# Layer 2's shifted rows in transfers of 60, 2 and 63 rows, long shifts first, and its fourth ring cleared by ScalarE

## The chip, the cores and the metric

The kernel runs on one core of one Trainium2 chip. The metric is the device time of one execution in microseconds. A core has TensorE (PE; its weight loads are listed as PEld), VectorE (DVE), ScalarE (ACT), GpSimd (POOL) and SyncE (SP). In this kernel SP issues nearly all direct transfers, which 16 DMA engines carry out.

## The reference

Four layers follow each other on x of shape (4, 256, 64, 64), float32. Each takes the group-normalized x and adds its result to x:

```
x = x + L0(gn(x))   # modulated deformable 3x3 convolution
x = x + L1(gn(x))   # attention over the 4096 places
x = x + L2(gn(x))   # DCNv4: sampled 3x3 windows in 16 groups of 16 channels
x = x + L3(gn(x))   # a Mamba block, scanned along the 4096 places
```

The change lies in layer 2:

```
xp   = einsum('bchw,oc->bhwo', x, w_value) + b_value
off, mask = split(einsum('bchw,oc->bhwo', x, w_om) + b_om)    # 9 points a group
val  = bilinear samples of the zero-padded xp at (y + ky + off_y, x + kx + off_x)
out  = einsum('bhwkgc,bhwgk->bhwgc', val, mask)
x   += einsum('bhwc,oc->bohw', out, w_out) + b_out
```

## The kernel before

Images go one after the other, and within an image the layers too. Layer 2 takes no gather. It assumes that no offset is over one place (a flag sends the program to another version else), so each output place needs only the 5 x 5 places around it. For every place and group a table `A` of 5 x 5 weights is built from mask and offsets, and the output is the sum of 25 products of weights and shifted values.

The 128 partitions hold two half images: partition 64h + x is column x of half h. Rows are taken two at a time, in 16 steps p (`T = 2`). The projected values of two rows (a "ring" of shape 128 x 5 x 2 x 256) are made by PE (`values`, L754 and L756). Then `spread` copies them by ACT into the middle of five places (L762), and fills the other four by transfers from SBUF to SBUF that shift by d = -2, -1, 1, 2 partitions within each half (L766). A shift by 1 moves 63 partitions, a shift by 2 moves 62, each with one contiguous row of 2 KB, so a spread has eight transfers. The partitions that a shift leaves out must hold zero, which is why the four rings are cleared at the start of each image's layer 2: two by POOL (L739), the third by ACT (L741), the fourth by POOL (L945).

Step p uses rings p, p+1 and p+2. Three spreads go out at the start, ring p+3 is spread during step p, and the last one, ring 17, during step 14. Step p does, for the five window rows wy and two rows t:
- `product` (L888 on DVE, L893 on POOL): DVE multiplies five places at once for t = 0 and wy < 4, and otherwise three (shifts -2, -1, 0), with POOL doing the other two (shifts 1, 2);
- `shares` (L875, L876) on ACT, a copy of weights for POOL's part;
- for the next step `masked` (L803), `outer` (L823, on POOL) and `gather` (L836), which build the next `A`;
- `pairs` (L902) on POOL, one addition, and `total` (L913) on PE, which sums the remaining places by transposes into PSUM.

`project` (L852) and `finish` (L864) on PE and DVE close a step two steps later.

PE, ACT, DVE and POOL keep the order in which the code of the steps is written (`manual_schedule`), so a waiting instruction holds up all that stands behind it on its engine. What stands before that block, such as the normalization (`scaled`, L201, on DVE) and the clearing of the first three rings, is put into order by the framework. SP issues transfers in order, too. Eight completion semaphores take turns on SP, and an issue waits until the transfer eight places earlier has landed.

Of the kernel before, what the change touches and what calls it, by code (L numbers as in the profile page):

```python
# [63 lines left out]
class Net:  # L64
# [635 lines left out]
    def layer2(self, x):  # L700
# [3 lines left out]
        nc, tc = self.nc, self.tc  # L704
        gk, T = GRP * K2, 2
        with (
# [27 lines left out]
            ring = []  # L734
            for i in range(4):

                r = pa.tile([P, WIN, VR, 256], F32, tag=f"ring{i}", name=f"ring{i}")
                if i < 2:
                    nc.gpsimd.memset(r, 0.0)  # L739
                elif i == 2:  # L740
                    nc.scalar.copy(  # L741
                        r.rearrange("p x y c -> p (x y c)"), zero.to_broadcast([P, WIN * VR * 256])
                    )
                ring.append(r)

            def values(q, pool=None):

                r = ring[q % 4]
                pc = pool.tile([P, 512], F32, tag="pacc", name="pc3") if pool else self.ps("pc2")
                for u in range(VR):  # L750
                    y = VR * q + u
                    o = pc[:, bass.ts(u, 256)]
                    for ct in range(2):
                        nc.tensor.matmul(o, xr[:, ct, y, :], wv[:, ct, :], start=(ct == 0), stop=False)  # L754
                    k = 1 if y < 2 else 2 if y >= HH + 2 else 0
                    nc.tensor.matmul(o, self.halves[:, k, :], bv, start=False, stop=True)  # L756
                return pc

            def spread(q, pc):

                r = ring[q % 4]
                nc.scalar.copy(r[:, 2].rearrange("p y c -> p (y c)"), pc)  # L762
                for d in (-2, -1, 1, 2):
                    for h in range(2):
                        a, b = 64 * h + max(0, -d), 64 * h + 64 - max(0, d)
                        nc.sync.dma_start(out=r[a:b, 2 + d, :, :], in_=r[a + d : b + d, 2, :, :])  # L766


            made = {}
# [1 line left out]
            def offsets(p, t):  # L771

                if t == 0:
                    made.setdefault(p, {})["po"] = pom.tile([P, T, 512], F32, tag="pom", name="pom")
                po = made[p]["po"]
                for ct in range(2):
                    nc.tensor.matmul(
                        po[:, t, : 3 * gk], xr[:, ct, T * p + t + 2, :], wom[:, ct, :], start=(ct == 0), stop=False
                    )
                nc.tensor.matmul(po[:, t, : 3 * gk], self.halves[:, 0, :], bom, start=False, stop=True)  # L780

            def hats(p, part):


                d = made[p]
                po = d["po"][:, :, : 2 * gk]
                if part == 0:
                    d["hat"] = pb.tile([P, 2 * gk, T, 3], F32, tag="hat", name="hat")
                    d["ab"] = pb.tile([P, T, 2 * gk], F32, tag="ab", name="ab", bufs=1)
                side = lambda i: d["hat"][:, :, :, i].rearrange("p k t -> p t k")  # L790
                if part == 0:
                    nc.scalar.activation(side(0), po, AF.Relu, scale=-1.0)
                    nc.scalar.activation(side(2), po, AF.Relu)
                    nc.scalar.activation(d["ab"], po, AF.Abs)
                else:
                    nc.scalar.activation(side(1), d["ab"], AF.Identity, bias=1.0, scale=-1.0)

                    nc.scalar.activation(d["ab"], d["ab"], AF.Relu, bias=-1.0, accum_out=seen[:, p : p + 1])

            def masked(p):  # L800
                d = made[p]
                d["mh"] = pb.tile([P, gk, T, 3], F32, tag="mh", name="mh")
                nc.vector.tensor_mul(  # L803
                    d["mh"],
                    d["hat"][:, 0:gk],
                    d["po"][:, :, 2 * gk : 3 * gk]
                    .rearrange("p t (k u) -> p k t u", u=1)
                    .to_broadcast([P, gk, T, 3]),
                )

            def clear(p):
                A = pshare.tile([P, 1024], F32, tag="A", name="A")[:, : GRP * T * WIN * WIN]
                nc.scalar.copy(A, zero.to_broadcast([P, GRP * T * WIN * WIN]))
                made.setdefault(p, {})["A"] = A.rearrange("p (g t y x) -> p g t y x", t=T, y=WIN, x=WIN)

            def outer(p, i, engine):

                d = made[p]
                if i == 0:
                    d["pr"] = pb.tile([P, gk * T, 3, 3], F32, tag="pr", name="pr", bufs=1)  # L820
                mh, hat = (d[n].rearrange("p k t i -> p (k t) i") for n in ("mh", "hat"))
                n = gk * T // 3
                engine.tensor_mul(  # L823
                    d["pr"][:, bass.ts(i, n)],
                    mh[:, bass.ts(i, n), :].rearrange("p k (y x) -> p k y x", x=1).to_broadcast([P, n, 3, 3]),
                    hat[:, bass.ds(gk * T + i * n, n), :]
                    .rearrange("p k (y x) -> p k y x", y=1)
                    .to_broadcast([P, n, 3, 3]),
                )
# [94 lines left out]
            with tc.manual_schedule(  # L924
                engines={
                    mybir.EngineType.PE,
                    mybir.EngineType.Activation,
                    mybir.EngineType.DVE,
                    mybir.EngineType.Pool,
                }  # L930
            ):
                clear(0)
                for t in range(T):
                    offsets(0, t)
                hats(0, 0)
                spread(0, values(0))
                hats(0, 1)
                spread(1, values(1, pacc))
                masked(0)
                for i in range(3):  # L940
                    outer(0, i, nc.vector)
                spread(2, values(2))
                for t in range(T):
                    offsets(1, t)
                nc.gpsimd.memset(ring[3], 0.0)  # L945
                for i in (0, 2, 1):
                    gather(0, i)
                hats(1, 0)
                hats(1, 1)


                behind = None
                for p in range(last + 1):
                    near, far = p < last, p < last - 1
                    for wy in range(WIN):
                        product(p, wy, 0)
                        if wy == 0:
                            shares(p)
                        if near and wy == 0:
                            masked(p + 1)  # L960
                        product(p, wy, 1)
                        if wy == 1 and p > 1:
                            finish(p - 2)
                        if near and wy > 1:
                            gather(p + 1, wy - 2)
                        if near and wy < 3:
                            outer(p + 1, wy, nc.gpsimd)
                        left = pairs(p, wy)
                        if behind:
                            total(*behind)  # L970
                        behind = p, wy, made[p]["prod"], left
                        if wy == 0:
                            if p:
                                turned(p - 1)
                            if near:
                                clear(p + 1)
                        if far and wy < 2:
                            offsets(p + 2, wy)
                        if wy == 2:
                            if far:  # L980
                                hats(p + 2, 0)
                            if p < last:
                                spread(p + 3, values(p + 3))
                        if wy == 3:
                            if far:
                                hats(p + 2, 1)
                        if wy == 4:
                            if p:
                                project(p - 1)
                total(*behind)  # L990
                nc.scalar.preload_act_table_set("sqrt_and_others")
                turned(last)
                finish(last - 1)
                project(last)
                finish(last)
# [853 lines left out]
```

## Time and profile before

| | |
|---|---|
| three runs | 9211.65, 9220.24, 9221.78 us, median 9220.24 |
| the profiled execution | 9224.37 us, its span 9222.6 us |
| granted TensorE clock | 0.967 |
| busy in the span | PE 8204.3 us (89%), DVE 7308.7 (79%), POOL 6976.5 (76%), ACT 4967.0 (54%) |
| layer 2, fourth image | from about 7916 to 8255 us of the span |
| L766, SP, ring<-ring | 576 transfers, 569/767/2512 ns min/median/max for an issue |
| L893, POOL | 384 instructions, median 1072 ns |
| L888, DVE | 640 instructions, 936 to 1492 ns |
| L739 and L945, POOL clearing a ring | 2231 ns each, and 2377 ns |
| L741, ACT clearing a ring | 2323 ns |

A line of the timeline gives the start and the length in us, the engine, the line of the kernel, the operation, the tiles written and read, their shapes and the number of instructions merged into it; in brackets stands the engine's idle time just before it and what ended that. "us" in the issue of a transfer is the time that it takes on SP, not the time until the data has landed. Shares of the whole span say little here, since the four layers have different limits; what bounds layer 2 has to be read in its own stretch.

### The profile page before, as it was taken

What the parts mean: (1) busy time and instruction counts of PE and PEld (TensorE: products, weight loads), DVE (VectorE), ACT (ScalarE), POOL (GpSimd) and SP (SyncE); (2) the same over time, 40 slices, a digit from 0 to 9 for tenths busy, and PEclk for the clock granted to TensorE, in tenths of its full rate; (3) what the DMA queues carried; (4) which work ended last, traced back from release to release, by engine and by line L of the source; (5) the groups of instructions that cost most, each with busy time, mean ns of one, the idle gap of its engine ahead of it and who ended that gap; (6) DMA issues with size and microseconds to landing.
All of it is one profiled execution on the core that took longest, in us unless ns stands there. A gap on an engine that the chain in (4) does not pass through costs nothing. (4 is left out here: it accounts for less than half of the span.)

```text
span 9222.6 us, 95498 instructions
## 1 busy us (share of the span) xinstructions
PE 8204.3 (89%) x32023; PEld 4337.2 (47%) x32023; DVE 7308.7 (79%) x8245; ACT 4967.0 (54%) x7717; POOL 6976.5 (76%) x4224
## 2 busy tenths in 40 slices
PE   5889898998888989899888898999988889889997
PEld 4643473443564346344356435634435633564443
DVE  5864498999786458999978645899997854689998
ACT  4843336666684333666668333366666833336664
POOL 4746697998674669799867467889986746788997
PEclk9999999999999999999999999999999999999999
DMA  8930011222892011122389101112248900111221
GB/s 301 356 120 1 29 58 59 67 67 82 288 360 90 1 34 61 56 66 66 100 297 359 61 1 39 59 57 67 66 121 311 349 33 1 43 61 53 63 63 51
DMA packets 409192, 1017.79 MB, mean 110 GB/s; under 512 B 38833, under 2 KB 106834, under 8 KB 406642
## 3 DMA queue, kind: packets, MB, share of 16 engines
q0 software_dynamic: 165888, 604.05, 17.5%
q1 hardware_dynamic: 242802, 407.54, 14.4%
q8 instruction: 255, 4.18, 0.2%
q14 instruction: 247, 2.02, 0.1%
HBM read 849.60 MB, written 88.10 MB: 102 GB/s over the span
## 5 line engine op out<-in xcount | busy, mean ns | idle before, releaser
L1704 POOL TENSOR_TENSOR h<-h,cn 128x2048 f32<-128x2048 f32 x508 | 2300.4, 4528 | 41.1 <-POOL carry L1701 0.2
L1681 DVE TENSOR_TENSOR_SCAN h<-da,carry,h 128x512 f32<-128x512 f32 x1800 | 2175.2, 1265 | 85.0 <-ACT da L1679 36.8
L1679 ACT ACTIVATE da<-delta,l3a 128x512 f32<-128x512 f32 x2048 | 1395.7, 689 | 1206.4 <-DVE h L1681 1202.7
L1561 PE MATMUL y<-h,ident 128*128 128x512 f32 x4096 | 1923.7, 603 | 14.8 <-POOL h L1704 14.8
L371 POOL DMA_INDIRECT g<-tab,idx x1152 | 1337.0, 1161 | 515.3 <-DVE r L380 131.3
L592 POOL TENSOR_TENSOR acc<-acc,e 128x1024 f32<-128x1024 f32 x480 | 1125.4, 2345 | 540.0 <-ACT e L588 518.8
L1561 PEld LDWEIGHTS y<-h,ident 128*128 128x128 f32 x4096 | 787.7, 194 | 1067.6 <-issue 975.9
L415 PE MATMUL pz<-cols,l0w 128*128 128x256 f32 x4608 | 1154.8, 395 | 30.2 <-DVE cols L404 24.5
L489 DVE TENSOR_REDUCE m<-pm 128x3 f32<-128x1536 f32 (+2 forms) x340 | 599.5, 1763 | 699.6 <-PE pm L479 699.6
L380 DVE SCALAR_TENSOR_TENSOR r<-g,wx,r 128x512 f32<-128x512 f32 x1152 | 862.2, 748 | 238.0 <-ACT r L379 230.5
L588 ACT ACTIVATE e<-sc 128x1024 f32<-128x1024 f32 x512 | 496.1, 1020 | 1029.4 <-PE sc L575 1025.2
L1598 DVE TENSOR_TENSOR h<-du,bn 128x2048 f32<-128x2048 f32 (+1 forms) x512 | 1025.9, 2004 | 4.0 <-PE bn L1583 3.9
L599 PE MATMUL cx<-e,v 128*128 128x512 f32 x2048 | 1000.2, 616 | 0.0
L379 ACT ACTIVATE r<-g,wx 128x512 f32<-128x512 f32 x1152 | 830.0, 720 | 283.1 <-DMA g<-tab,idx 230.9
L415 PEld LDWEIGHTS pz<-cols,l0w 128*128 128x128 f32 x4608 | 857.9, 196 | 179.3 <-DVE cols L404 79.4
L888 DVE TENSOR_TENSOR prod<-ring,A 128x768 f32<-128x768 f32 (+1 forms) x640 | 716.6, 1161 | 90.0 <-DMA ring<-ring 59.3
L913 PE MATMUL pacc<-ident,prod 128*128 128x128 f32 x5120 | 678.8, 284 | 75.7 <-POOL prod L893 41.7
L397 PE MATMUL pt<-ident,acc 128*128 128x128 f32 x2304 | 437.2, 290 | 264.3 <-DVE acc L388 261.3
L913 PEld LDWEIGHTS pacc<-ident,prod 128*128 128x128 f32 x5120 | 576.7, 144 | 164.9 <-POOL prod L893 62.2
L599 PEld LDWEIGHTS cx<-e,v 128*128 128x128 f32 x2048 | 352.3, 189 | 599.0 <-issue 596.4
L387 ACT ACTIVATE acc<-r,wy 128x256 f32<-128x256 f32 x1152 | 569.2, 494 | 4.2 <-DVE r L380 3.1
L388 DVE SCALAR_TENSOR_TENSOR acc<-r,wy,acc 128x256 f32<-128x256 f32 x1152 | 551.7, 479 | 2.4 <-ACT acc L387 2.0
(272 smaller groups left out, 11488.7 us busy)
## 6 DMA issues: line engine op xcount, KB each, us to landing
cn<-cd SPq DMA_DIRECT2D x512, 256.0 KB
bs<-cd SPq DMA_DIRECT2D x248, 256.0 KB
tab<-vtnext SPq DMA_DIRECT2D x96, 512.0 KB
ring<-ring SPq DMA_DIRECT2D x288, 126.0 KB
ring<-ring SPq DMA_DIRECT2D x288, 124.0 KB
g<-tab,idx POOLq DMA_INDIRECT x1152, 6.3
tab<-vt SPq DMA_DIRECT2D x28, 640.0 KB
x<-in_x SPq DMA_DIRECT2D x64, 256.0 KB
```

What stands on the lines that cost most here:

```text
L371: nc.gpsimd.indirect_dma_start(out=g[:], out_offset=None, in_=tab[:, :], in_offset=bass.IndirectOffsetOnAxis(ap=idx[:, t, k : k + 1], axis=0),
L379: nc.scalar.mul(r, g[:, :, 0, :], wx[:, 0, t, k : k + 1])
L380: nc.vector.scalar_tensor_tensor(r, g[:, :, 1, :], wx[:, 1, t, k : k + 1], r, ALU.mult, ALU.add)
L415: nc.tensor.matmul(sums[m][:, ot, :256], wf[:, i, bass.ts(ot, P)], cols[m][:, i, :], start=(i == 0), stop=(i == 17),)
L592: nc.gpsimd.tensor_add(b["acc"], b["acc"], e)
L599: nc.tensor.matmul(blocks[qb]["cx"], v[:, 4 * (i + kt // 4 * 4) + kt % 4, :], e[:, bass.ts(i % 2, 512)], start=(kt == 0 and i == 0), stop= ...
L913: nc.tensor.matmul(d["pd"][:, ct, t, :], prod[:, x, t, bass.ts(ct, P)], self.ident, is_transpose=True, start=(wy == 0 and x == left[0] and ...
L1561: nc.tensor.matmul(c["ys", dc], self.ident, h[:, dc, :], start=False, stop=(n == DS - 1))
L1598: nc.vector.tensor_mul(h[:, :d, :], c["du"][:, :d, :], c.pop(("bn", n)).to_broadcast([P, d, C]))
L1679: nc.scalar.activation(da, c["delta"][:, dc, :], AF.Exp, scale=al[:, dc, n : n + 1])
L1681: nc.vector.tensor_tensor_scan(h[:, dc, :], da, hb, carry[:, dc, n : n + 1], ALU.mult, ALU.add)
L1704: nc.gpsimd.tensor_mul(h, h, cn.to_broadcast([P, 4, C]))
```

## The change

The two shifts by 2 are each cut into one transfer of 60 partitions and one of 2, for both halves; the shifts by 1 stay as they were. A spread then has twelve transfers for eight. Both long shifts are issued ahead of the short ones. The fourth ring is cleared by the same ACT copy as the third, ahead of the block with the fixed order, and POOL's memset in that block is gone. In ACT's program the new copy stands behind the square root of the normalization (L189) and ahead of the first clearing of `A` (L813). Lines from L767 on move down by one, and those behind L945 stay.

```
@@ -737,7 +737,7 @@
                 r = pa.tile([P, WIN, VR, 256], F32, tag=f"ring{i}", name=f"ring{i}")
                 if i < 2:
                     nc.gpsimd.memset(r, 0.0)
-                elif i == 2:
+                else:
                     nc.scalar.copy(
                         r.rearrange("p x y c -> p (x y c)"), zero.to_broadcast([P, WIN * VR * 256])
                     )
@@ -760,10 +760,11 @@
 
                 r = ring[q % 4]
                 nc.scalar.copy(r[:, 2].rearrange("p y c -> p (y c)"), pc)
-                for d in (-2, -1, 1, 2):
+                for d in (-2, 2, -1, 1):
                     for h in range(2):
                         a, b = 64 * h + max(0, -d), 64 * h + 64 - max(0, d)
-                        nc.sync.dma_start(out=r[a:b, 2 + d, :, :], in_=r[a + d : b + d, 2, :, :])
+                        for lo, hi in ((a, b),) if d % 2 else ((a, a + 60), (a + 60, b)):
+                            nc.sync.dma_start(out=r[lo:hi, 2 + d, :, :], in_=r[lo + d : hi + d, 2, :, :])
 
 
             made = {}
@@ -942,7 +943,6 @@
                 spread(2, values(2))
                 for t in range(T):
                     offsets(1, t)
-                nc.gpsimd.memset(ring[3], 0.0)
                 for i in (0, 2, 1):
                     gather(0, i)
                 hats(1, 0)
```

More of the change, by code (lines that the diff above doesn't have):

```diff
@@ L739, in layer2 @@
                     nc.gpsimd.memset(r, 0.0)
-                elif i == 2:
+                else:
                     nc.scalar.copy(
@@ L762, in spread @@
                 nc.scalar.copy(r[:, 2].rearrange("p y c -> p (y c)"), pc)
-                for d in (-2, -1, 1, 2):
+                for d in (-2, 2, -1, 1):
                     for h in range(2):
                         a, b = 64 * h + max(0, -d), 64 * h + 64 - max(0, d)
-                        nc.sync.dma_start(out=r[a:b, 2 + d, :, :], in_=r[a + d : b + d, 2, :, :])
+                        for lo, hi in ((a, b),) if d % 2 else ((a, a + 60), (a + 60, b)):
+                            nc.sync.dma_start(out=r[lo:hi, 2 + d, :, :], in_=r[lo + d : hi + d, 2, :, :])
             made = {}
@@ L944, in layer2 @@
                     offsets(1, t)
-                nc.gpsimd.memset(ring[3], 0.0)
                 for i in (0, 2, 1):
```

## The prediction

> **What bounds the kernel now.** I read the busy shares first, then layer 2's stretch of the last image by windows, then GpSimd's instructions at both ends of it, then the DMA view. All four images look alike here, so the fourth stands for them.
>
> Stretches of layer 2: start, first rows, middle, end; columns are length, busy time of PE, PEld, DVE, ACT, POOL, the granted clock, the DMA share and GB/s:
>
> ```profile
> 7917.00:7933.00 16.00, 9.86 (x28) 5.25 (x28) 12.41 (x27) 8.00 (x10) 6.88 (x4) 0.68 0.19 69
> 7933.00:7980.60 47.60, 29.05 (x123) 18.00 (x122) 29.83 (x38) 14.38 (x23) 17.55 (x15) 0.78 0.24 78
> 7980.60:8193.00 212.40, 210.35 (x1307) 157.99 (x1305) 203.92 (x272) 86.49 (x147) 212.40 (x171) 1.00 0.19 59
> 8193.00:8251.00 58.00, 46.86 (x292) 37.92 (x291) 43.80 (x58) 10.68 (x21) 45.39 (x38) 0.91 0.14 43
> ```
>
> In the middle POOL is busy all 212.40 us: it is the bound, one pair of rows every 17.5 us, and no transfer is on the path. In the first 47.6 us it works 17.55 us. What it waits for, at the start and at the end:
>
> ```profile
> 7951.78 1.06 POOL L893 TENSOR_TENSOR prod<-ring,near 128x512 f32<-128x512 f32 x1 [27.91 <-ACT near L876]
> ...
> 7962.60 1.06 POOL L893 TENSOR_TENSOR prod<-ring,near 128x512 f32<-128x512 f32 x1 [6.79 <-DMA ring<-ring]
> ...
> 7975.08 1.06 POOL L893 TENSOR_TENSOR prod<-ring,near 128x512 f32<-128x512 f32 x1 [4.47 <-DMA ring<-ring]
> ...
> 7980.60 1.07 POOL L893 TENSOR_TENSOR prod<-ring,near 128x512 f32<-128x512 f32 x1
> ```
> ```profile
> 8236.07 1.28 POOL L902 TENSOR_TENSOR prod<-prod 128x512 f32<-128x512 f32 x1 [0.19 <-DVE prod L888]
> 8241.15 1.06 POOL L893 TENSOR_TENSOR prod<-ring,near 128x512 f32<-128x512 f32 x1 [3.81 <-DMA ring<-ring]
> ```
>
> DVE has such a wait of 7.25 us too, before its first product at 7949.83 (it is what delays 7951.78). So the shifted rows bound both ends, 4 times. Why they are slow, in the last spread alone (issued from 8224.55 to 8232.1):
>
> ```profile
> GB/s 0 0 0 0 26 0 0 0 0 23 16 66 92 82 108 157 118 82 128 134 92 46 52 52 49 52 46 52 49 52 49 26 13 0 0 0 0 0 0 0
> DMA packets 545, 1.04 MB, mean 42 GB/s; under 512 B 44, under 2 KB 44, under 8 KB 544
> ...
> ring<-ring SPq DMA_DIRECT2D x4, 126.0 KB
> ring<-ring SPq DMA_DIRECT2D x4, 124.0 KB
> ```
>
> 500 rows of 2 KB make 500 packets; the 44 small ones are completion marks, one per DMA engine and transfer: 4a + 4b = 44. The trace puts 2 marks on a 62-row transfer and 9 on a 63-row one, the largest divisors of 62 and 63 up to 16. For 6 us the queue runs at some 51 GB/s: two engines, 31 rows each, 0.080 us a row. All 62-row transfers sit on the same two engines: 4 x 31 + 4 x 7 = 152 rows, 12.2 us a spread. Three spreads back to back give the landings 7949.6, 7962.4, 7974.8, which are the waits above.
>
> Last, a collision ahead of all this:
>
> ```profile
> 7920.63 3.02 DVE L201 TENSOR_SCALAR xr<-x,gm,rs 128x256 f32<-128x256 f32 x2
> 7921.13 2.38 POOL L945 MEMSET ring<- 128x2560 f32 x1
> ```
>
> The second of the two DVE instructions takes 2.39 us under the memset of the fourth ring; the same form takes 0.39 to 0.45 just after. PE's first layer-2 matmul (7924.28) waits for it. Image one shows 2.39 at the same place.
>
> **The fourth ring on ScalarE.** Taken from POOL: 2.38 us that nobody waits for except that DVE instruction, so 2.39 - 0.40 = 2.0 us come off the path. Added to ACT: 2.32 us (the third ring's copy there), behind the root at 7920.06 in ACT's order, so the normalization is not delayed. Its cover is ACT's idle time before L792: 6.49 to 7.90 us in the four images; less 2.32 and less the 2.0 by which L792 comes earlier, some 2 to 3 us stay. Without that cover it would cost its 2.32. The small POOL step L1130 (0.40 us) now falls later beside L201; at most 0.4, off the path.
>
> **Rows as 60 + 2.** By the divisor pattern 60 rows go over 15 engines, 4 rows each, and 2 rows over 2. The busiest engine then has 4 x 4 + 4 x 1 + 4 x 7 = 48 rows, 3.9 us a spread for 12.2. The engines stop being the bound, and SP's issuing becomes it: 12 issues for 8. The queue waits of up to 2.5 us inside an issue (569/767/2512 ns min/median/max on L766) come from the two full engines and go.
>
> Price of an issue. 63 rows: 0.70 to 0.77 (no queue wait); I take 0.73. 60 rows: no row; 62 rows on 2 engines cost 0.57 and 63 on 9 cost 0.70 to 0.77, and stretched to 15 engines this gives 0.81 to 0.94; a 128-row load costs 0.32. I take 0.85, since only the ring rows go from SBUF to SBUF. 2 rows: from 0.27 (a 3-row load) to 0.57 (62 rows); I take 0.45. A spread: 4 x (0.85 + 0.45 + 0.73) + 12 x 0.045 between issues = **8.7 us**, ends 5.7 and 9.7. Landing: a 62-row transfer alone took 5.39, less 31 x 0.08 = 2.9 fixed, so 63 rows land 3.45 after issue. With s for a spread, ring n is complete (n+1)s + 2.65 after SP's first issue. SP's queue holds nothing else here. Each issue waits for the landing of the one eight places earlier; eight issues (5 us) are longer than 3.45.
>
> The Trainium skill (DMA: Bandwidth & Descriptors, "Why a DMA increments its semaphore by 16 and not by 1") says that a transfer takes the largest number of engines up to 16 that divides its slowest dimension: 15 for 60 rows. No run here shows that value yet.
>
> **Long shifts first.** DVE's three-wide products need shifts -2 and -1; the -1 rows now come tenth of twelve: issued 6.3 after the spread's start, landed at 9.8. It enters below.
>
> **Start, from SP's first issue (7932.99).** POOL reaches the second row pair at 7980.60, 47.6 later. Three paths lead there now:
> - POOL from the first ring: s + 2.85, then 1.95 (7949.83 to 7951.78), 4.0, 8.0, 5.5 of own work: s + 22.3 = 31.0.
> - POOL from the third: 3s + 2.85 + 5.5 (7975.08 to 7980.60) = 34.5.
> - DVE from the third: 2s + 9.9, 5.56 (7968.62 to 7974.18), 1.95: 2s + 17.4 = **34.8**.
>
> The last is longest: 47.6 - 34.8 = 12.8 us. Next late is POOL itself at 17.5 a pair. DVE's lead over it is 1.95 instead of 6.4, but it was 1.95 to 4.4 in the middle as well while POOL never waited, and DVE alone needs 16.86.
>
> **End.** The last ring lands at 8224.55 + 8.7 + 2.65 = 8235.9, and POOL is free at 8237.3: the 3.81 goes. After that idle time PE ran 15 transposes in 3.46 us and 8 matmuls in 3.02, for 1.9 and 1.7 when busy; up to 3 us of this goes as well, until POOL's last sum binds. I take 6.0, between 3.8 and 6.9.
>
> **Sum.** 2.0 + 12.8 + 6.0 = 20.8 an image, 83 in all. The profiled execution took 9224.4 (span 9222.6 and 1.8 around it): 9141. The median of the runs is 4.1 lower: **9137**. With s = 5.7 the start gives 18.8 and the end 6.9: 111, so 9109. With s = 9.7 and an end of 3.8: 10.1 + 2.0 + 3.8, 64, so 9156. Beyond the rows, at s = 11, the start gives 6.2 and the end 3.0: 45, so 9175.
>
> **Rivals.**
> - *Given back.* DVE comes only 8.3 earlier to its second row pair (34.8 - 1.95 against 41.2), and its 16.86 can't build up the lead, so POOL waits for DVE: 2.0 + 8.3 + 3.8 = 14 an image, 9164. For: DVE is 96% busy in the middle. Against: 17.5 against 16.86.
> - *It doesn't do what it says.* 60 rows stay on two engines: 120 + 4 + 28 rows, 152 as before. Only the collision goes: 8 us, 9212, no change that can be told. Against: 9 engines for 63 rows.
> - *Slower: issuing takes the DMA's place.* At the start the change loses from 3s + 8.35 = 47.6, s = 13.1, which is 1.05 us an issue. At s = 16 (1.3 an issue; an issue does reach 1.8 in the last spread) the start loses 8.8, the end 2.3 (ring at 18.7 against 16.3), less 2.0: 9 an image, 9256. For: half more issues on one queue. Against: every 62-row issue with a free queue takes 0.57 to 0.67.
>
> The Trainium skill (the same page, "Rules for kernel authors") speaks against the split: under 64 KB a transfer pays mostly overhead, and the 2-row ones are 4 KB. If each added its fixed 2.9 in series, s would be 8.7 + 11.6 = 20 and this last rival would be far worse; but here transfers issued 0.6 apart overlap.
>
> **How the numbers follow.** Forecast 0.72, given back 0.18, no effect 0.05, slower 0.05. A measurement of this kernel tells 0.2% (18 us) from no change. Faster 0.90, same 0.05, slower 0.05. The range reaches from 9109 over "given back" to 9176, which takes in issues somewhat dearer than the rows make them; no effect and slower are left out.
>
> **What would show it.** Right: L201's longest near 0.7 us in layer 2; 15 marks for each 60-row transfer, no 51 GB/s plateau; a spread's 12 issues in about 8.7 us; POOL's waits for the rings under 3 us each at the start and none at the end; POOL still without a gap in the middle. Wrong: issues of 60 rows above 1.2 us, or POOL waiting for DVE between the ends.

## The result and the profile after

The changed kernel takes 9140.83 us (median of six runs, 9135.43 to 9168.87), the kernel before 9220.14 us on the same chip: ratio 0.9922 (95% interval 0.9911 to 0.9933), 79 us less. The prediction was 9137. The profiled execution of the changed kernel took 9168.87 us, the longest of its six: layers 0 and 1, which the change does not touch, took 951.7 to 963.1 us an image in it (from layer 0's first gather to layer 2's first scaled rows) and 943.7 to 955.9 in the profile before, together 23.5 us more. So layer 2 is compared stage by stage.

Windows of the changed kernel's last image, the same four stretches as before (length, busy PE, PEld, DVE, ACT, POOL, granted clock, DMA share, GB/s):

```profile
7881.00:7896.00 15.00, 10.47 (x27) 5.46 (x28) 10.77 (x28) 10.08 (x10) 9.21 (x6) 0.65 0.20 73
7896.00:7932.60 36.60, 26.09 (x125) 16.21 (x123) 26.13 (x35) 14.70 (x24) 17.63 (x15) 0.91 0.32 98
7932.60:8145.00 212.40, 210.39 (x1307) 157.97 (x1304) 207.04 (x276) 86.43 (x147) 212.40 (x170) 1.00 0.19 59
8145.00:8201.00 56.00, 47.01 (x300) 37.83 (x298) 46.49 (x64) 10.90 (x21) 45.69 (x39) 0.94 0.17 53
```

The second stretch shrank from 47.6 to 36.6 us with the same 17.6 us of POOL's work in it. The third is unchanged: POOL busy all the time. The bounds of the first and the last are too rough to show what these lost. Over all four images, worked out from the two traces (us, mean of an image):

| stage of layer 2 | before | after | change | predicted |
|---|---|---|---|---|
| first scaled rows to SP's first ring issue | 13.11 | 11.07 | -2.04 | -2.0 |
| from there to POOL's second row pair ("start") | 47.47 | 36.50 | -10.97 | -12.8 |
| 14 steps in the middle | 249.68 | 249.69 | 0 | 0 |
| first to last product of POOL in step 15 ("end") | 13.91 | 10.26 | -3.65 | |
| from there to layer 3's first shift ("tail") | 14.57 | 12.92 | -1.65 | -6.0 with the end |
| sum | 338.73 | 320.43 | -18.3 | -20.8 |

Four images make 73.2 us of the 79.3. A repeat of the changed kernel (below) gave 319.96 an image. Layer 3, up to the next image's first gather, went from 986.6 to 985.2 us an image, which would be 5.6 us more; in the kernels of this study it varied from 982.8 to 986.8 with no edit in it, so no cause is claimed.

POOL at the start of the changed kernel, from its timeline. The brackets are POOL's idle time and what ended it:

```profile
7910.52 1.06 POOL L894 TENSOR_TENSOR prod<-ring,near 128x512 f32<-128x512 f32 x1 [16.51 <-ACT near L877]
...
7917.76 1.06 POOL L894 TENSOR_TENSOR prod<-ring,near 128x512 f32<-128x512 f32 x1 [3.22 <-issue]
...
7927.02 1.06 POOL L894 TENSOR_TENSOR prod<-ring,near 128x512 f32<-128x512 f32 x1 [1.24 <-PE pacc L914]
...
7932.58 1.06 POOL L894 TENSOR_TENSOR prod<-ring,near 128x512 f32<-128x512 f32 x1
```

and at the end:

```profile
8188.09 1.28 POOL L903 TENSOR_TENSOR prod<-prod 128x512 f32<-128x512 f32 x1 [0.17 <-DVE prod L889]
8189.33 1.06 POOL L894 TENSOR_TENSOR prod<-ring,near 128x512 f32<-128x512 f32 x1
```

The idle times of 27.91, 6.79 and 4.47 at the start became 16.51, 3.22 and 1.24, and the 3.81 at the end is gone. At 7927.02 the profile names PE, but the third ring's last rows landed at 7926.69, 0.33 us ahead of it, and in all images of both kernels this product starts 0.16 to 0.33 us behind that landing: the ring still sets this place. PE's slow work at the end is gone too. Before, in the chain of waits of the last image:

```profile
8242.26 3.46 PE pacc L913 x15
8245.72 3.02 PE pz L852 x8
```

and now:

```profile
8190.44 1.90 PE L914 MATMUL pacc<-ident,prod 128*128 128x128 f32 x15 [0.25 <-POOL prod L894]
8192.18 1.89 PE L853 MATMUL pz<-oT,l 128*128 128x256 f32 x8
```

It goes with the granted clock. Behind 4.09 us in which PE waited for POOL's product, the clock was 0.50 over the 15 transposes and 0.59 over the 8 matmuls; now PE is idle for 0.25 us, and the clock is 1.00 over both.

The DMA view around the last spread (8173 to 8198):

```profile
GB/s 0 0 0 0 26 0 0 0 193 10 125 79 0 164 39 82 121 16 164 118 144 157 121 102 3 0 0 0 0 0 0 0 0 0 0 0 0 0 0 0
DMA packets 605, 1.04 MB, mean 42 GB/s; under 512 B 104, under 2 KB 104, under 8 KB 604
...
ring<-ring SPq DMA_DIRECT2D x4, 126.0 KB
ring<-ring SPq DMA_DIRECT2D x4, 120.0 KB
ring<-ring SPq DMA_DIRECT2D x4, 4.0 KB
```

The plateau at 51 GB/s is gone. 104 completion marks are 4 x 15 + 4 x 2 + 4 x 9: 60 rows went over 15 engines. SP's issuing is what remains. The chain of waits shows one spread transfer by transfer, with start and length of each:

```profile
7905.66 0.79 SPq L767
7906.50 0.64 SPq L767
7907.18 0.83 SPq L767
7908.05 0.64 SPq L767
7908.73 0.83 SPq L767
7909.60 0.64 SPq L767
7910.28 0.83 SPq L767
7911.16 0.64 SPq L767
7911.84 0.76 SPq L767
7912.64 0.70 SPq L767
7913.39 0.70 SPq L767
7914.13 0.70 SPq L767
7914.93 0.79 SPq L767
```

60 and 2 rows take turns, then come four of 63. From 7905.66 to 7914.93 a spread takes 9.27 us, with some 0.05 us between issues. A transfer of 2 rows costs 0.64 us, three quarters of one of 60.

### The profile page after: what moved, and what is told of

Same layout as the page of the kernel before. It is cut to its first block, busy times and chain, and to the rows that moved or that the text cites. A ratio compares the mean times of both kernels' runs of the same rounds, so it can differ in the third digit from the quotient of the medians.

```text
span 9167.1 us, 95918 instructions
## 1 busy us (share of the span) xinstructions
PE 8177.5 (89%) x32023; PEld 4309.4 (47%) x32023; DVE 7300.7 (80%) x8245; ACT 4979.0 (54%) x7721; POOL 7007.6 (76%) x4220
## 3 DMA queue, kind: packets, MB, share of 16 engines
q14 instruction: 249, 2.04, 0.1%
## 5 line engine op out<-in xcount | busy, mean ns | idle before, releaser
L371 POOL DMA_INDIRECT g<-tab,idx x1152 | 1359.4, 1180 | 516.1 <-DVE r L380 127.7
L914 PE MATMUL pacc<-ident,prod 128*128 128x128 f32 x5120 | 665.8, 280 | 46.3 <-POOL prod L903 17.9
```

The source lines that it names most:

```text
L371: nc.gpsimd.indirect_dma_start(out=g[:], out_offset=None, in_=tab[:, :], in_offset=bass.IndirectOffsetOnAxis(ap=idx[:, t, k : k + 1], axis=0),
L914: nc.tensor.matmul(d["pd"][:, ct, t, :], prod[:, x, t, bass.ts(ct, P)], self.ident, is_transpose=True, start=(wy == 0 and x == left[0] and ...
```

## Experiments

Ten more kernels ran, and the changed one once more. The first four shared a chip on which the kernel before took 9447 us, the next four one with 9221 us and the last three one with 9212 us, so times are compared as ratios to the kernel before on the same chip, and stages from the traces. Means of four images, in us; "sum" runs from the first scaled rows to layer 3's first shift:

| kernel | rows | start | middle | end | tail | sum | ratio, 95% interval |
|---|---|---|---|---|---|---|---|
| before | 13.11 | 47.47 | 249.68 | 13.91 | 14.57 | 338.73 | 1 |
| after | 11.07 | 36.50 | 249.69 | 10.26 | 12.92 | 320.43 | 0.9922 (0.9911 to 0.9933) |
| clearing alone | 11.07 | 47.38 | 249.87 | 13.91 | 14.11 | 336.35 | 0.9997 (0.9987 to 1.0006) |
| split alone | 12.60 | 34.91 | 249.69 | 10.25 | 12.74 | 320.20 | 0.9928 (0.9915 to 0.9940) |
| order alone | 13.06 | 48.95 | 253.41 | 14.62 | 14.44 | 344.47 | 1.0028 (1.0017 to 1.0039) |
| without the 2 rows | 11.06 | 30.84 | 249.87 | 10.25 | 12.75 | 314.77 | 0.9896 (0.9882 to 0.9910) |
| 30 + 30 + 2 rows | 10.70 | 46.39 | 249.74 | 13.35 | 13.54 | 333.73 | 0.9986 (0.9976 to 0.9995) |
| half issued by GpSimd | 11.03 | 30.80 | 249.86 | 10.27 | 12.86 | 314.81 | 0.9887 (0.9873 to 0.9901) |
| after, old order | 11.08 | 34.91 | 249.69 | 10.29 | 12.74 | 318.71 | 0.9916 (0.9903 to 0.9929) |
| 32 + 30 rows | 11.19 | 35.43 | 249.87 | 10.25 | 12.65 | 319.39 | 0.9926 (0.9913 to 0.9939) |
| GpSimd and old order | 10.86 | 30.77 | 249.64 | 10.28 | 12.84 | 314.39 | 0.9888 (0.9873 to 0.9904) |
| that, copies on DVE | 10.89 | 29.91 | 249.66 | 10.28 | 12.93 | 313.67 | 0.9893 (0.9878 to 0.9908) |
| after, again | 10.63 | 36.48 | 249.67 | 10.26 | 12.92 | 319.96 | 0.9919 (0.9906 to 0.9933) |

"Rows" is the time from the first scaled rows to SP's first ring issue; in the four images of the kernel before it lies between 12.36 and 13.64, so half a microsecond there is no effect.

**The clearing alone.** The kernel before with only this part of the change:

```
-                elif i == 2:
+                else:
...
-                nc.gpsimd.memset(ring[3], 0.0)
```

> The kernel before, with only the fourth ring's clearing moved to ScalarE; transfers as before. Theory (three separate parts: full DMA engines at both ends, and the memset that holds up one DVE instruction): only the collision goes, 1.3 to 2.4 us an image, so 5 to 10 us off the 9220, with L201's longest in layer 2 near 0.65 us and POOL's waits for the rings unchanged (about 15 us an image). Rival 'collision': the memset is what costs most, and 40 us or more go. Rival 'order': nothing changes beyond the same 5 to 10.

The trace gives 2.4 us an image, 9.5 in all, 2.04 of it ahead of the first issue. The median fell by 5.9 us, which the timing can't tell from nothing.

**The split alone.** The order and the memset of before stay:

```
-                        nc.sync.dma_start(out=r[a:b, 2 + d, :, :], in_=r[a + d : b + d, 2, :, :])
+                        for lo, hi in ((a, b),) if d % 2 else ((a, a + 60), (a + 60, b)):
+                            nc.sync.dma_start(out=r[lo:hi, 2 + d, :, :], in_=r[lo + d : hi + d, 2, :, :])
```

> The kernel before, with only the 62-row transfers cut into 60 and 2; old order of the shifts, the fourth ring cleared by GpSimd as before. Theory: the two full engines are the cause, so the gain of the start (11.2 us an image) and of the end (6.2) comes whole: 65 to 73 us off, a spread issued in 9.3 us, POOL at its second pair of rows 36 to 37 us after SP's first issue. Rival 'order': without the long shifts first, under 20 us. Rival 'collision': under 40.

18.5 us an image and 73 us by the medians: the split brings as much alone as the whole change. The start is 1.6 us shorter than in the changed kernel. The third ring's last rows tell why: there they landed 11.76 us after their spread's first issue, here 10.29. The last transfer of the spread is now one of 2 rows, landed 1.75 us after its issue, and not the fourth in a row of 63 rows on the same nine engines, landed 3.3 after its own. DVE gains as well: it starts on the third ring 26.0 us after SP's first issue, for 29.0 in the changed kernel, where the -1 rows go out tenth of twelve.

**The order alone.**

```
-                for d in (-2, -1, 1, 2):
+                for d in (-2, 2, -1, 1):
```

> The kernel before, with only the order of the shifts changed to -2, 2, -1, 1; 62 and 63 rows in one transfer each, clearing as before. Theory: the two engines carry the same 152 rows a spread, so the last row lands when it did; the -1 rows land later, for which DVE's three-wide products wait: between no change and 10 us slower. Rival 'order': 50 us or more faster.

23 us slower, more than either theory allowed. The wait list of this kernel (us in all, times, longest), where the kernel before has 59.3 us in 15 waits for DVE and 58.6 in 12 for POOL:

```profile
DVE prod L888 <- DMA ring<-ring: 123.2, 45, 8.5
POOL prod L893 <- DMA ring<-ring: 63.3, 12, 6.9
```

With all four 62-row transfers ahead, DVE waits for its -1 rows in 30 places more, and the middle, which no transfer had touched so far, grows by 3.7 us an image. POOL's idle time in the middle grows from 4.3 to 7.8 us an image, so 3.5 of the 3.7 are there. The profile names nothing for the longest of these waits, but the timeline shows what ends them:

```profile
8311.67 0.29 ACT L875 COPY near<-A 128x160 f32<-128x160 f32 x1 [5.33 <-DVE prod L888]
8311.86 0.19 ACT L876 COPY near<-A 128x32 f32<-128x32 f32 x1
8312.09 1.06 POOL L893 TENSOR_TENSOR prod<-ring,near 128x512 f32<-128x512 f32 x1 [1.92 <-issue]
```

POOL's first product of a pair starts 0.04 us behind ACT's copy of its weights, ACT waits for DVE's first product of that pair, and DVE is late. All added waits but one of 0.25 us end this way.

**Without the 2-row transfers.** From the changed kernel:

```
-                        for lo, hi in ((a, b),) if d % 2 else ((a, a + 60), (a + 60, b)):
+                        for lo, hi in ((a, b),) if d % 2 else ((a, a + 60),):
```

> The changed kernel without the 2-row transfers, so that two edge places of each half keep zeros for the shifts by 2 (part of the computation is left out); it asks what those four issues of a spread cost. Theory (SP's issuing is the bound at the start of the changed kernel): a spread is issued in 9.27 - 4 x 0.68 = 6.6 us, POOL's second pair starts 2s + 17.4 = 30.6 after SP's first issue for 36.4, the end stays: some 23 us below the changed kernel, near 9117. Rival 'landing' (what bounds the start is the time to land, or the engines, not the issuing): within 8 us of the changed kernel, near 9140.

The start falls to 30.84 us, near the 30.6 expected, but not by the path that was expected:

```profile
8098.48 1.06 POOL L894 TENSOR_TENSOR prod<-ring,near 128x512 f32<-128x512 f32 x1 [15.51 <-ACT near L877]
...
8115.99 1.05 POOL L894 TENSOR_TENSOR prod<-ring,near 128x512 f32<-128x512 f32 x1
```

From 8098.48 to 8115.99 POOL works without a gap. No transfer is on the path any more, and that 30.84 is so close to the sum for DVE's path (2s + 17.4) is luck. With the 4 KB transfers gone a spread takes 6.4 to 6.7 us to issue: they cost 2.6 to 2.9 us of every spread, and 5.7 of the start until POOL's own work bounds it. In the changed kernel SP's queue is the bound.

**30 + 30 + 2 rows.** The opposite: as many rows, more issues.

```
-                        ... ((a, a + 60), (a + 60, b)):
+                        ... ((a, a + 30), (a + 30, a + 60), (a + 60, b)):
```

> The changed kernel with each 60-row transfer cut into 30 and 30: the busiest engine's rows stay (2 + 2 for 4), but a spread has sixteen issues. Theory (SP's issuing bounds the start): each 30-row issue costs about what a 60-row one does, 0.8, so a spread takes 9.27 + 4 x 0.83 = 12.6, the start about 3s + 8.7 = 46.5 for 36.5, the end 2 to 3 us more: 45 to 55 us above the changed kernel, 0.25 to 0.35% below the kernel before. Rival 'rows': the cost of an issue goes with its rows, a spread stays near 9.5, and the time within 10 us of the changed kernel's.

The start is 46.39 for an expected 46.5: nearly all of the start's gain goes, with the engines as evenly loaded as before. The trace agrees with the expected distance to the changed kernel, 13.3 us an image or 53 in all; the ratio to the kernel before does not, 0.14% for an expected 0.25 to 0.35%. The issues of this kernel (number, ns min/median/max), then of the one without the 2-row transfers:

```profile
L767 SPq DMA_DIRECT2D ring<-ring x1152: 630/779/2062, 1072.2 to 8212.0; - x192
```
```profile
L767 SPq DMA_DIRECT2D ring<-ring x576: 697/779/1564, 1128.7 to 8366.0; - x192
```

30 rows cost 0.78 us behind another 30, and 0.83 behind a 2-row transfer. 60 rows cost the same: 0.78 behind another 60, in the kernel without the 2-row transfers, and 0.83 behind 2 rows in the changed kernel. Both go over 15 engines. The price does not follow the rows.

**32 + 30 rows.** Is it the number of engines, then? Two transfers for each shift by 2 as in the changed kernel, over 16 and 15 engines.

```
-                        ... ((a, a + 60), (a + 60, b)):
+                        ... ((a, a + 32), (a + 32, b)):
```

> The changed kernel with the 62 rows cut into 32 and 30 instead of 60 and 2. Theory (an issue costs more with more engines: 0.64 for 2, 0.70 for 9, 0.83 for 15): 32 rows on 16 engines cost about 0.85 and 30 on 15 engines 0.83, so a spread takes 4 x 0.2 more, 10.1, the start 39 for 36.5: 8 to 14 us above the changed kernel. Rival 'power of two': 32 rows are issued in 0.35 like a 32-row store of the kernel, a spread takes 8.1, and the time falls by 10 to 15 us.

32 rows over 16 engines cost 0.56 us and 30 over 15 cost 0.78. So neither rows nor engines set the price alone; the theory fell, and the rival had the direction right but not the size (0.56 for 0.35). A spread takes 8.8 us for 9.27, and the sum falls by 1.0 us an image, which the timing can't tell.

**Half of the issuing by GpSimd.** For the three spreads at the start, ahead of which POOL is idle for 16.5 us:

```
-                            nc.sync.dma_start(out=r[lo:hi, 2 + d, :, :], in_=r[lo + d : hi + d, 2, :, :])
+                            (nc.gpsimd if h and q < 3 else nc.sync).dma_start(out=r[lo:hi, 2 + d, :, :], in_=r[lo + d : hi + d, 2, :, :])
```

> The changed kernel with the second half image's six transfers of the first three spreads issued by GpSimd, which stands idle there, so that SP and GpSimd share the issuing. Theory: SP's half takes 4.6 us a spread and GpSimd's about 6 (some 1.0 an issue, as its gathers take), so the start falls from 36.5 to 28 to 31 and the end stays: 22 to 34 us below the changed kernel. Rival 'landing': the last row's landing time or GpSimd's own issuing takes the place, and the time stays within 8 us of the changed kernel's, or above it.

9111.07 us, 110 less than before. GpSimd's 72 issues (ns min/median/max) and its first products of the last image:

```profile
L767 POOL DMA_DIRECT2D ring<-ring x72: 511/521/626, 1068.7 to 7861.5; - x72
```
```profile
7863.76 1.06 POOL L894 TENSOR_TENSOR prod<-ring,near 128x512 f32<-128x512 f32 x1 [1.76 <-ACT near L877]
...
7881.28 1.07 POOL L894 TENSOR_TENSOR prod<-ring,near 128x512 f32<-128x512 f32 x1
```

From 7863.76 to 7881.28 POOL works 17.52 us without a gap, 17.5 being its own work for a pair of rows. No transfer bounds the start any more; what does is the first product, held by ACT's copy of the weights. The same floor of 30.8 showed without the 2-row transfers.

**The changed kernel with the old order.**

```
-                for d in (-2, 2, -1, 1):
+                for d in (-2, -1, 1, 2):
```

> The changed kernel with the shifts in the old order -2, -1, 1, 2. Theory (from the split alone, whose start took 34.9 for 36.5): a short last transfer lands sooner than a 63-row one, so 1.6 us an image go at the start, and DVE's three-wide products get their rows sooner: 5 to 9 us below the changed kernel, 0.83 to 0.88% below the kernel before. Rival 'order helps': 5 us or more above the changed kernel.

1.7 us an image less than the changed kernel by the trace, 7 in all, as expected; the intervals of the ratios overlap.

**GpSimd and the old order together**, the last two edits at once:

> The changed kernel with two edits at once: the old order of shifts, and half 1 of the first three spreads issued by GpSimd. The theory: with GpSimd issuing, the spreads no longer set the start (GpSimd works 17.5 us without a gap from its first near product, which waits for ScalarE's copies, to the second row pair), so the order has nothing left to give there: start 30.8 us as with the split alone, total of layer 2 up to layer 3 within 1.5 us an image of 314.8, ratio 0.988 to 0.9895 to the kernel before. The rival: the order's 1.7 us an image add to it, 313.1 an image and 7 us less (ratio 0.9875 or less).

Start 30.77 and sum 314.39: the order gives nothing once POOL is at its floor. The time is 9113.89 us, 99 below the kernel before and 22 below the changed kernel on this chip; the 25 to 36 expected were too many, while the traces say 5.6 an image, which is 22.

**In addition the copies on DVE**, for the first pair of rows (and likewise the second copy, L877):

```
-                nc.scalar.copy(d["near"][:, :WIN], ...)
+                (nc.scalar.copy if p else nc.vector.tensor_copy)(d["near"][:, :WIN], ...)
```

> The kernel of the run before it, and in addition the three copies that fill the near rows of the first row pair go from ScalarE to VectorE. The theory (GpSimd's first near product, 13.3 us after the images' first scaled rows, waits for those copies behind ScalarE's hats): the first near product comes at about 11.6, the start goes from 30.8 to about 29.3 us, 5 to 7 us off the time. The rival: something else holds the start at 30.8, no change against the run before it.

```profile
7859.72 1.06 POOL L894 TENSOR_TENSOR prod<-ring,near 128x512 f32<-128x512 f32 x1 [1.04 <-DVE near L876]
7861.15 1.79 POOL L824 TENSOR_TENSOR pr<-mh,hat 128x864 f32<-128x864 f32 x1 [0.36 <-DVE mh L804]
```

Two copies were moved, not three. The first product does come 1.5 us earlier (11.8 after the first issue for 13.3), so ACT's copies did set the floor. But DVE, having made the copies, now delays `masked`, and POOL waits 0.36 us for that. It reaches the second pair at 7877.79, 18.07 us after its first product (17.9 to 18.3 in the four images) and not 17.52. The start falls by 0.86 us and not 1.5, the sum by 0.7 an image, and the time (9113.77) not at all that can be told. 5 to 7 us were expected.

**The changed kernel again**, beside those two:

> The changed kernel as it is, so that the two runs above and it are compared on one chip: ratio to the kernel before 0.991 to 0.993, 70 to 80 us less; the kernel with both edits 25 to 36 us below it.

9136.25 us, 76 less than the kernel before. Its trace has layer 2 at 75 us less.

## Why the prediction was right, point by point

- **The collision**: predicted 2.0 us an image, measured 2.04, and the same with this part alone. The longest scaling of layer 2 takes 0.65 us in the changed kernel, 2.39 before. The cover on ACT held: 3.47 to 3.75 us of its idle time before L793 are left, for the 2 to 3 predicted.
- **Engines**: 15, 2 and 9 marks and no plateau, as worked out from the divisors. The Trainium skill's rule for the number of engines (DMA: Bandwidth & Descriptors, "Why a DMA increments its semaphore by 16 and not by 1") holds for 60 rows, and in the experiments for 30 (15) and 32 (16). Rows on the busiest engine no longer matter: the start follows the issuing, 35.4 us at 8.8 a spread, 36.5 at 9.27 and 46.4 at 12.57.
- **The price of an issue** is the term that was mis-sized. 60 rows were taken at 0.85 and cost 0.83, 63 at 0.73 and cost 0.70, but 2 rows were taken at 0.45, between 0.27 and 0.57, and cost 0.64, above the upper row. Four of them made the spread 9.27 us for 8.7. That the range of the spread (5.7 to 9.7) held it is owed to its other terms.
- **The start**: measured 36.5 us for 34.8 predicted. With 9.27 in place of 8.7 the prediction's two late paths give 35.9 over DVE (2s + 17.4) and 36.2 over POOL (3s + 8.35). The prediction took the one over DVE. In the trace the two end together. At POOL's second pair, 7932.58:

```profile
7930.63 1.49 DVE L889 TENSOR_TENSOR prod<-ring,A 128x1280 f32<-128x1280 f32 x1
7931.30 1.28 POOL L903 TENSOR_TENSOR prod<-prod 128x512 f32<-128x512 f32 x1
7932.34 0.19 ACT L877 COPY near<-A 128x32 f32<-128x32 f32 x1
```

From DVE's product to POOL's it is 1.95 us in all four images, as predicted. POOL's own work ends at 7932.58 as well; in the other three images POOL idles 0.06 to 0.22 us there and waits for ACT's copy, so DVE's path is the later one by that little. The half microsecond above 35.9 is in two terms of it: two spreads took 18.73 us, since the first takes 9.47, and the third ring's -1 rows landed 10.1 us after their spread's start, not 9.8. With s = 12.6, from 30 + 30 + 2 rows, POOL's path gives 46.2 for 46.39 measured. One sign that the prediction named was missed by little: POOL waits 2.85 to 3.46 us for the second ring, and under 3 was said.

- **Long shifts first** was put into the sum at no net price. It has one: 1.6 us an image at the start with the split, and 5.7 in layer 2 without. The step that failed on POOL's path is the fixed 2.9 us of landing, read from one form and used for all, which makes it the same whichever transfer comes last: 2 rows land 1.75 us after their issue, 60 rows about 2.5, and of four transfers of 63 rows on the same nine engines the first 2.6 and the last 3.3. On DVE's path the prediction did count the late -1 rows, but it never worked out the old order, in which DVE starts on the third ring 3.0 us earlier and is off the path.
- **The end**: 5.3 us with the tail, for 6.0 (3.8 to 6.9). POOL waits for no ring there, as predicted.
- **Given back** did not happen: the middle is unchanged to 0.01 us. DVE's lead over POOL starts at 1.95 us and is back to 4.4 by the fifth step.
- **Slower by issuing** had the right mechanism and fell by its price: it needed 13.1 us a spread, and 30 + 30 + 2 rows, at 12.6, came within 15 us of the kernel before.
- **A rule against the split**: the Trainium skill (DMA: Bandwidth & Descriptors, "Rules for kernel authors") says that under 64 KB a transfer is mostly overhead. The runs bear it out for the issue, 0.64 us for 4 KB beside 0.70 for 126 KB. They don't for the landing, which overlapped: 12 transfers landed within 11.83 us of the first issue.

The sum was 83 us for layer 2 and came to 73. The median of the runs, 9140.8, lies 3.8 above the forecast. That it is so near is in part luck: 6 of the 10 missing microseconds were made up outside layer 2 by something that these runs don't explain.

## What to carry to other kernels

Count a transfer's engines from its completion marks before counting its bytes, and add up all transfers that use the same few engines: four at two engines each, beside four at nine, made 152 rows on two of sixteen. Once the engines are even, count issues: a small one costs nearly what a large one does (0.64 us for 2 rows, 0.70 for 63), and the next gain is a second issuing engine that is idle just then, not a finer split. Put last what lands soonest after its issue, but not what another engine needs first, and when a bound moves away, look for the engine's own work without a gap: beyond that no faster transfer helps.

## What was not expected of the hardware

- **Prices of an issue on SP**, contiguous 2 KB rows, median: 32 rows on 16 engines 0.56 us, 62 on 2 0.57 (with a free queue), 2 on 2 0.64, 63 on 9 0.70, 30 on 15 and 60 on 15 each 0.78 behind their like and 0.83 behind 2 rows. Neither the rows nor the engines order them; what does stays open.
- **GpSimd issues for less than SP**: 0.51 us for 2 rows, 0.53 for 63 and 0.54 for 60, where about 1.0 was expected. Its transfers land later, 4.0 us (median) after their issue, for 1.75 to 3.3 on SP. The Trainium skill (DMA: Bandwidth & Descriptors, "Rules for kernel authors") says that spreading transfers over issuing engines saves issue time only; that is what it did here, and issue time was the bound.
- **The collision has another direction.** In the changed kernel a small POOL instruction falls beside DVE's run of scalings (7885.12 to 7893.8):

```profile
L1130 POOL TENSOR_SCALAR l3a<-l3a x4: 4579/4581/4583, 1069.4 to 7889.4; 128x64 f32<-128x64 f32 x4
```

It took 0.40 us before (0.51 in the first image) and takes 4.58 now, in all four images. It lies over ten of DVE's 20 scalings and ends 0.23 us behind the last. Before the change DVE waited for POOL's memset, now, by these times, POOL waits for DVE, and only the first had somebody behind it. The Trainium skill (SBUF — State Buffer, "Who interferes with whom") has one exclusive pair of ports for the two, held by whoever starts first; both directions agree with that, though POOL's wait covers ten instructions of DVE and not one. The prediction put at most 0.4 us here.
